# A fourth buffer for the tail's turned contexts, and a reordered last stage, in a two-layer cross-attention kernel

## The chip, the cores and the metric

The kernel runs on one core of a Trainium2 chip, in one launch. The metric is the device time of that launch in microseconds. Three runs of the kernel before took 968.51, 970.0 and 969.3 us: the median is 969.3 us. All times below are in microseconds unless another unit is named; times inside the launch count from the start of the profiled span.

A core has five engines with queues of their own, each working in the order of its queue: TensorE (PE in the profile, its weight loads PEld), VectorE (DVE), ScalarE (ACT), GpSimd (POOL) and SyncE (SP). SP computes nothing; it issues most of the DMA transfers. ACT and POOL can issue transfers too. Sixteen DMA engines carry them all.

## The reference

The model is two layers over 16 batches of 112 rows of 256 numbers, with a context of 375 rows of 256 for each batch. All inputs are float32 except int8 weights at the very end.

```
x = x + attention16(layernorm(x), ctx, Wq, Wk, Wv, Wo) + bo      # 16 heads of 64
x = x + routed_ffn(layernorm(x)) + shared_ffn(layernorm(x))      # top-1 of 2 experts, 1024 hidden
e = layernorm(x) @ ctx.T / 16 - (1 - mask) * 1e9                 # one head, keys and values are ctx
x = x + softmax(e) @ ctx
n = layernorm(x)
x_scale = max(max|n| / 127, 1e-5)                                # over ALL rows of all batches
q = clip(round(n / x_scale), -128, 127)
x = x + (q @ weight_int8.T) * x_scale * weight_scale + bias
```

The last layer can't be finished for any batch before the maximum over all 16 batches is known: `x_scale` is one number for everything. This comparison and what follows it form the end of the kernel.

## The kernel before, in words

**Stages.** The first attention runs in 64 units (16 batches times 4 groups of heads). Beside it, in the free places of the units, the feed-forward layer and the second attention of batches 0 to 7 are done. Routing sorts the rows by expert in two halves; the second half of the rows is sorted at the end of the first attention and computed in eight slots of 128 rows. Units are numbered on: the slots are units 70 to 77 (`FIRST_RUN` = 70), then the steps of the tail begin, `STEP_0` = 82, in which batches 8 to 15 (`TAIL` = 8) pass through the second attention and the last norm. `at(u, f, ...)` puts a call at the end of unit u, `mid(u, ...)` in its middle; calls of one unit keep the order in which they were put. This order is written out by hand, and each engine's queue follows it.

**Slots.** In each slot unit `slot_run` computes 128 rows with one expert's weights and `slot_store` (L823) stores the result, `yrow`, to the sorted array `y_s` in DRAM, on SP's queue. The last slot is unit 77. Units 78 to 81 hold the four quarters of the shared layer's last chunk (`quarter(6, i)`, `acc_sh` and `ph_sh` in the profile), which keep TensorE busy to 901.3. Then `shared_store` (L804) writes that chunk's rows to DRAM on SP's queue, and `load_xs` (L809) loads the rows of batches 13, 14 and 15 from there, one each in steps 0, 1 and 2.

**Gathers.** For each tail batch `sort_get` (L829) gathers its expert rows from `y_s` into `got`, an indirect DMA issued by POOL. It must wait for all eight slots' stores. The gathers of batches 8 to 11 come in steps -4 and -3, one right behind the other on POOL, then `sort_add` (L843) on POOL adds them, and `norm` follows: statistics on DVE (L271, L272), root on POOL (L275, L276), negated mean on POOL (L286), the normed rows `xn` on ACT (L300).

**A batch in the tail.** `stages(k)` writes step k for all batches that are under way; batch b = 8 + k is the one whose scores are computed in step k. Its own steps are:

- `second_1`, one step ahead: TensorE turns the normed rows (`pt_x`, L327), ACT copies them to `xT2` (L330).
- `second_2`, step k: TensorE computes the scores `pe` (L857) from `xT2` and the turned context `ctxT2`; ACT scales and masks them to `e` (L862), DVE finds the maxima (L871), ACT takes the exponentials (L878).
- `second_3`, a step later: the probabilities are turned (`pp`, L460).
- `second_4`, two steps later: TensorE multiplies them by the natural context `ctx_nat` (`pa`, L888), DVE adds the result to x (L897). Then come the statistics of the last norm (`l3`).
- three steps later: the rows of the last norm on ACT, and `third_max`: DVE's largest absolute value of the batch (`amax`, L925) and POOL's addition of the bias (L928).
- four steps later: `third_turn` turns these rows into `x3T`, the operand of the last product.

**Contexts.** `load_ctxT2` (L128 to L130) loads a batch's turned context, 128 partitions of 750 numbers, 375 KB; `load_ctx` (L119) loads the natural one, 125 partitions of 3 times 256 numbers, also 375 KB. Both are issued by SP. `late(pool, 2, n, ...)` gives the tail n buffers: three for `ctxT2`, five for `ctx_nat`. Batches 8, 9 and 10 are loaded at the end of units 75, 76 and 77, each pair behind that unit's `slot_store`; step k of the tail then loads batch 11 + k (`do(-3, ...)`, from step 0). A load waits, at the head of SP's queue, until its buffer's former reader is done: batch b's turned context reuses the buffer of batch b - 3. In unit 83 (step 1) SP also loads `x3T` of batches 0 to 7 (L1244, 896 KB), which were turned earlier and kept in DRAM.

**The end.** In step 9 (`k == B - TAIL + 1`) DVE reduces the maxima of batches 0 to 14 to `amax1`. Batch 15, the last, is compared by a short way on DVE (`farthest`, L314 to L317) without waiting for its normed rows; L1331 joins the two, TensorE turns the column (`pm`, L1333), DVE takes the maximum of the line (`top`, L1335), TensorE broadcasts it (`pb`, L1338), DVE makes `xscale` and `rscale` (L1340, L1342). Between `pm` and `pb` stand two idle products (`keep_warm(2)`, L1231), which only keep TensorE busy. After that comes the last call of `stages`, step 10, which turns batch 14's columns and writes batch 15's normed rows, and `third_turn` for batch 15.

Then the 16 batches are quantised in eight pairs: `scaled` multiplies by `rscale` and adds a constant that rounds, on ACT (L1355) for pairs 1, 3, 5, 6, 7 or on DVE (L1357) for pairs 0, 2, 4; `products` takes the constant off again to bf16 `xi` on ACT (L1362) and multiplies (`pf`, L1366); `stored` multiplies by the scales on DVE into `y` (L1377, four buffers), adds x on DVE for pairs 2, 5, 7 or on POOL for the others (L1385), and SP stores the pair (L1386). `y` of pair p reuses the buffer of pair p - 4 and so waits for that pair's store to land.

Of the kernel before, what the change touches and what calls it, by code (L numbers as in the profile page):

```python
# [19 lines left out]
P = 128  # L20
B, S, D = 16, 112, 256
SK = 375
# [4 lines left out]
DC = D // P  # L27
# [27 lines left out]
TAIL = 8  # L55
# [3 lines left out]
def tile_kernel(  # L59
# [26 lines left out]
    nc = tc.nc  # L86
# [4 lines left out]
    ctxp = ctx.enter_context(tc.tile_pool(name="ctx", bufs=2))  # L91
# [10 lines left out]
    def gen(name):  # L102
        return ps_gen.tile([P, 512], F32, tag="gen", name=name)
# [13 lines left out]
    ctx_nat, ctxT, ctxT2 = {}, {}, {}  # L117
# [8 lines left out]
        dma.dma_start(out=ctxT[b], in_=ctx_t[b])  # L126

    def load_ctxT2(b):  # L128
        ctxT2[b] = late(ctxp, 2, 3, [P, DC, SK], "ctxT_2", f"ctxT2_{b}")
        nc.sync.dma_start(out=ctxT2[b], in_=ctx_t[b])  # L130

    def weight(src, name, dma, pool=wpool):
# [112 lines left out]
    def late(pool, bufs, more, shape, tag, name):  # L245

        pool, bufs = (fin[0], more) if fin else (pool, bufs)
        return pool.tile(shape, F32, tag=tag, name=name, bufs=bufs)
# [73 lines left out]
    def transposed(dst, src, name):  # L322

        pt = gen(f"pt_{name}")
        n = src.shape[0]
        for c in range(DC):
            nc.tensor.transpose(  # L327
                pt[:, c * n : (c + 1) * n], src[:, c * P : (c + 1) * P], ident[:n, :n]
            )
        nc.scalar.copy(dst, pt[:, : DC * n].rearrange("p (c s) -> p c s", c=DC))  # L330
# [523 lines left out]
    def second_2(b, between=lambda: None):  # L854
        pe = gen(f"pe_{b}")
        for dc in range(DC):
            nc.tensor.matmul(  # L857
                pe[:S, :SK], xT2[b][:, dc, :], ctxT2[b][:, dc, :], start=(dc == 0), stop=(dc == DC - 1)
            )
        e = late(tmp, 1, 2, [S, SK], "e", f"e_{b}")  # L860
        if b >= TAIL:
            nc.scalar.activation(  # L862
                e, pe[:S, :SK], AF.Identity, bias=negb[:, b : b + 1], scale=ESCALE
            )
        else:
            nc.vector.tensor_scalar(e, pe[:S, :SK], ESCALE, negb[:, b : b + 1], ALU.mult, ALU.add)
        between()
        nmax = small.tile([S, 1], F32, tag="nmax2", name=f"nmax2_{b}")
        if b >= TAIL:

            nc.vector.tensor_reduce(nmax, pe[:S, :SK], AX.X, ALU.max)  # L871
            nc.vector.tensor_scalar(
                nmax, nmax, -ESCALE, negb[:, b : b + 1], ALU.mult, ALU.subtract
            )
        else:
            nc.vector.tensor_reduce(nmax, e, AX.X, ALU.max, negate=True)
        den = small.tile([S, 1], F32, tag="den2", name=f"den2_{b}")
        nc.scalar.activation(e, e, AF.Exp, bias=nmax, accum_out=den)  # L878
        rdens[b] = den
        es[b] = e  # L880
# [32 lines left out]
    def third_turn(bs):  # L913
        for b in bs:
            if b < TAIL:
                t = tmp.tile([P, DC, S], F32, tag="x3s", name=f"x3s_{b}", bufs=1)
                transposed(t, normed["l3", b], f"x3_{b}")
                nc.scalar.dma_start(out=x3T_d[b], in_=t)
            else:
                transposed(x3T[0][:, b, :, :], normed["l3", b], f"x3_{b}")  # L920

    def third_max(bs):
        for b in bs:
            if b < B - 1:
                nc.vector.tensor_reduce(  # L925
                    amax[:, b : b + 1], normed["l3", b], AX.X, ALU.max, apply_absolute_value=True
                )
            nc.gpsimd.tensor_tensor(xs[b], xs[b], bias_bc[:S], ALU.add)  # L928
# [84 lines left out]
    STEP_0 = FIRST_RUN + NT // 2 + 5  # L1013
# [4 lines left out]
    def at(u, f, *a):  # L1018
        extra[u].append((f, a))
# [85 lines left out]
    for b in range(TAIL):  # L1105
        at(u - 2 - (b > 0), sort_get, b)
        at(u - 4, load_xs, b)
        at(u - 2, load_ctxT2, b)
        at(u - 1, load_ctx, b)
        mid(u - 1, sort_add, b)  # L1110
        mid(u, second_1, b)
        at(u, second_2, b)
        mid(u + 1, second_3, b)
        at(u + 1, second_4, b)
        at(u + 1, third_norm, [b])
        mid(u + 3, third, [b])
        u += 1
# [44 lines left out]
    for b in range(TAIL, B):  # L1162

        at(FIRST_RUN + 3 if b < 13 else STEP_0 + b - 13, load_xs, b)
    for i in range(3):
        at(STEP_0 - 7 + i, load_ctxT2, TAIL + i)
        at(STEP_0 - 7 + i, load_ctx, TAIL + i)

    make_kT(0, 0, True)
    for i in range(GB):  # L1170
# [56 lines left out]
    def keep_warm(count):  # L1227

        pi = gen("warm")
        for _ in range(count):  # L1230
            nc.tensor.matmul(pi[:, :P], ident, ident, start=True, stop=True)  # L1231
# [22 lines left out]
    def stages(k):  # L1254
        def b_of(back):
            b = TAIL + k - back
            return b if TAIL <= b < B else None

        def do(back, f):
            b = b_of(back)  # L1260
            if b is not None:
                f(b)

        def norm_steps(name, b):
            nb_on = nc.gpsimd if name == "l2" or b == B - 1 else nc.vector
            steps[name, b] = norm([b], name, True, nb_on)
            for f in steps[name, b][:3]:
                f()

        def now(f, at_k):  # L1270

            for b, own in zip(range(TAIL, B), at_k):
                if own == k:
                    f(b)

        def rows(name):
            return lambda b: steps[name, b][3]()

        no = None
        stats = lambda b: norm_steps("l2", b)  # L1280
        now(sort_get, (-4, -4, -3, -3))
        now(sort_add, (-3, -3, no, no, 1, 2, 3, 4))
        now(stats, (-2,))
        now(rows("l2"), (-1,))
        yield
        now(sort_add, (no, no, -2, -1))
        now(stats, (no, -2))
        if k == -1:
            now(rows("l2"), (no, -1))
            do(-1, second_1)  # L1290
        do(0, lambda b: second_2(b, lambda: do(-1, second_1)))
        do(4, lambda b: third_turn([b]))
        do(1, second_3)
        do(3, rows("l3"))
        now(rows("l2"), (no, no, 0, 1, 2, 3, 4, 5))
        do(2, second_4)
        if k == B - TAIL + 1:

            amax1.append(const.tile([S, 1], F32, tag="amax1", name="amax1"))
            do(3, lambda b: third_max([b]))  # L1300
            nc.vector.tensor_reduce(amax1[0], amax[:, : B - 1], AX.X, ALU.max)
        do(2, lambda b: norm_steps("l3", b))
        now(sort_get, (no, no, no, no, -1, 0, 1, 2))
        now(stats, (no, no, -1, 0, 1, 2, 3, 4))
        if k >= 0:
            do(-3, load_ctxT2)
            do(-3, load_ctx)
        if k != B - TAIL + 1:
            do(3, lambda b: third_max([b]))
        yield  # L1310

    for u in range(NU + 3, LAST - 1):
        for f, a in middle[u]:
            f(*a)
            pump(2)
        k = u - STEP_0
        part = stages(k)
        next(part)
        for f, a in extra[u]:
            f(*a)  # L1320
            pump(2)
        if k >= B - TAIL:
            keep_warm(4)
        next(part)
# [8 lines left out]
    nc.tensor.transpose(pm[:1, :S], amax1, ident[:S, :S])  # L1333
    top = const.tile([1, 1], F32, tag="top", name="top")
    nc.vector.tensor_reduce(top, pm[:1, :S], AX.X, ALU.max)  # L1335
    keep_warm(2)
    pb = gen("pb")
    nc.tensor.matmul(pb[:, :1], ones[0:1, :], top, start=True, stop=True)  # L1338
    xscale = const.tile([P, 1], F32, tag="xscale", name="xscale")
# [4 lines left out]
    for _ in stages(LAST - 1 - STEP_0):  # L1344
        pass
# [5 lines left out]
    def scaled(pair):  # L1351
        t = x3T[0][:, 2 * pair : 2 * pair + 2, :, :]

        if pair % 2 or pair == 6:
            nc.scalar.activation(t, t, AF.Identity, bias=rounding, scale=rscale)  # L1355
        else:
            nc.vector.tensor_scalar(t, t, rscale, ROUND, ALU.mult, ALU.add)  # L1357
# [17 lines left out]
    def stored(pair):  # L1375
        y = fin[0].tile([S, 2, D], F32, tag="y", name=f"y_{pair}", bufs=4)
        nc.vector.tensor_tensor(  # L1377
            y,
            pfs[pair][:S, : 2 * D].rearrange("p (j d) -> p j d", j=2),
            wsx.unsqueeze(1).to_broadcast([S, 2, D]),  # L1380
            ALU.mult,
        )
        first = xs_place[2 * pair]
        add = nc.vector if pair in (2, 5, 7) else nc.gpsimd
        add.tensor_tensor(y, y, xall[:S, first : first + 2, :], ALU.add)  # L1385
        nc.sync.dma_start(  # L1386
            out=out[2 * pair : 2 * pair + 2].rearrange("b s d -> s b d"), in_=y
        )

    NP = B // 2  # L1390
    scaled(0)
    scaled(1)
    for pair in range(NP + 1):
        if pair < NP:
            products(pair)
        if pair + 2 < NP:
            scaled(pair + 2)
        if pair > 0:
            stored(pair - 1)
# [59 lines left out]
```

## Time and profile before

| | us |
|---|---|
| median of three runs | 969.3 |
| the profiled execution's own time | 970.18 |
| its span, first to last instruction | 968.4 |
| TensorE busy in the span | 925.2 (96%) |
| DVE, ACT, POOL busy | 494.3, 465.9, 463.8 |
| granted TensorE clock, mean of the span | 0.986 |

TensorE is busy nearly throughout; its idle time lies at the end. A table of that end by stretches, from the trace (busy time of TensorE, granted clock, share of the DMA engines):

| stretch | long | PE busy | clock | DMA share |
|---|---|---|---|---|
| 880 to 890 | 10 | 10.00 | 1.00 | 0.57 |
| 890 to 900 | 10 | 9.71 | 1.00 | 0.29 |
| 900 to 907 | 7 | 5.48 | 1.00 | 0.35 |
| 907 to 920 | 13 | 6.70 | 0.90 | 0.88 |
| 920 to 930 | 10 | 9.81 | 0.79 | 0.53 |
| 930 to 940 | 10 | 9.33 | 1.00 | 0.17 |
| 940 to 950 | 10 | 5.38 | 0.74 | 0.00 |
| 950 to 968 | 18 | 6.00 | 0.69 | 0.33 |

How the page and the trace's answers are read: a line of the timeline or of the queue of SP has the start, the duration, the engine, the line of the kernel, the operation, the tiles (out<-in) and how often; in square brackets stands how long the engine was idle before and who ended that. A line of the chain of waits has start, duration and what the time went to. A line of a stretch has its bounds and length, then the busy time of PE, PEld, DVE, ACT and POOL with the number of their instructions, then the granted TensorE clock as a share of full speed, the mean busy share of the 16 DMA engines, and GB/s. In the page's slices each digit is a fortieth of the span, in tenths.

### The profile page before, as it was taken

What the parts mean: (1) busy time and instruction counts of PE and PEld (TensorE: products, weight loads), DVE (VectorE), ACT (ScalarE), POOL (GpSimd) and SP (SyncE); (2) the same over time, 40 slices, a digit from 0 to 9 for tenths busy, and PEclk for the clock granted to TensorE, in tenths of its full rate; (3) what the DMA queues carried; (4) which work ended last, traced back from release to release, by engine and by line L of the source; (5) the groups of instructions that cost most, each with busy time, mean ns of one, the idle gap of its engine ahead of it and who ended that gap; (6) DMA issues with size and microseconds to landing.
All of it is one profiled execution on the core that took longest, in us unless ns stands there. A gap on an engine that the chain in (4) does not pass through costs nothing. (4 is left out here: it accounts for less than half of the span.)

```text
span 968.4 us, 16839 instructions
## 1 busy us (share of the span) xinstructions
PE 925.2 (96%) x5567; PEld 706.4 (73%) x5567; DVE 494.3 (51%) x1276; ACT 465.9 (48%) x1241; POOL 463.8 (48%) x504
## 2 busy tenths in 40 slices
PE   8999999999999999999999999899999999999683
PEld 5677677777777777778778787667767678899462
DVE  5655855464545444653444434577576442322464
ACT  4766565366535554564353442554545641221453
POOL 4766664366536544553242334666555622201743
PEclk9999999999999999999999999999999999999996
DMA  5654543243326422332645522645335720586522
GB/s 185 161 164 95 136 129 74 71 101 92 74 74 197 121 70 52 77 83 59 217 159 179 205 50 70 161 127 139 95 77 133 201 59 30 201 325 220 151 96 76
DMA packets 119911, 120.69 MB, mean 125 GB/s; under 512 B 15807, under 2 KB 107153, under 8 KB 115089
## 3 DMA queue, kind: packets, MB, share of 16 engines
q1 hardware_dynamic: 107664, 97.52, 35.8%
q10 hardware_dynamic: 8144, 11.20, 4.0%
q0 software_dynamic: 4016, 10.90, 3.7%
q8 instruction: 45, 0.74, 0.3%
q14 instruction: 42, 0.34, 0.1%
HBM read 71.19 MB, written 10.62 MB: 84 GB/s over the span
## 5 line engine op out<-in xcount | busy, mean ns | idle before, releaser
L455 POOL TENSOR_SCALAR p<-p,rden 128x375 f32<-128x375 f32 x256 | 315.1, 1244 | 258.4 <-DVE rden L452 251.3
L443 ACT ACTIVATE p<-sc,nmax 128x375 f32<-128x375 f32 x256 | 143.4, 571 | 174.9 <-DVE nmax L434 169.6
L338 PE MATMUL pk<-ctxT,wk 128*128 128x375 f32 x512 | 192.1, 497 | 4.3 <-ACT kT L347 2.3
L359 PE MATMUL pv<-wv,ctxT 128*128 128x256 f32 (+1 forms) x768 | 187.0, 380 | 0.4 <-ACT kT L347 0.4
L359 PEld LDWEIGHTS pv<-wv,ctxT 128*128 128x128 f32 (+1 forms) x768 | 143.3, 187 | 47.9 <-ACT kT L347 1.6
L504 ACT COPY pT<-blk 32x384 f32<-32x384 f32 x256 | 130.0, 508 | 29.2 <-DMA pT<-blk 26.9
L476 DVE STREAM_TRANSPOSE blk<-p 128x384 f32<-128x384 f32 x256 | 132.2, 552 | 7.4 <-POOL p L455 4.5
L338 PEld LDWEIGHTS pk<-ctxT,wk 128*128 128x128 f32 x512 | 90.3, 191 | 55.7 <-issue 9.9
L434 DVE TENSOR_REDUCE nmax<-sc 128x2 f32<-128x750 f32 x128 | 111.8, 911 | 0.6 <-PE sc L426 0.5
L514 PEld LDWEIGHTS pa<-pT,v 128*64 128x64 f32 (+1 forms) x1536 | 74.4, 136 | 33.3 <-issue 15.8
L426 PE MATMUL sc<-kT,qT 64*128 64x375 f32 x512 | 98.1, 501 | 0.0
L514 PE MATMUL pa<-pT,v 128*64 128x112 f32 (+1 forms) x1536 | 88.3, 263 | 2.2 <-DMA pT<-blk 1.4
L372 DVE COPY v<-pv 119x256 f32<-119x256 f32 x64 | 27.0, 423 | 122.5 <-PE pv L359 101.3
L347 ACT COPY kT<-pk 128x375 f32<-128x375 f32 x128 | 61.3, 479 | 47.0 <-PE pk L338 47.0
L426 PEld LDWEIGHTS sc<-kT,qT 64*128 64x128 f32 x512 | 43.9, 186 | 34.1 <-issue 13.5
L770 DVE TENSOR_SCALAR hT_sl<-ph_sl,slot_b 128x128 f32<-128x128 f32 x64 | 22.3, 349 | 69.3 <-PE ph_sl L760 69.3
L760 PE MATMUL ph_sh<-ffn_x,sw 128*128 128x256 f32 x224 | 56.0, 381 | 0.0
L747 PE MATMUL acc_sh<-sw,hT_sh 128*128 128x256 f32 x224 | 55.5, 379 | 0.3 <-ACT hT_sh L772 0.3
L395 PE MATMUL pq<-xT,wq 128*128 128x224 f32 x256 | 54.2, 354 | 0.0
L772 ACT ACTIVATE hT_sl<-ph_sl,slot_b 128x128 f32<-128x128 f32 x64 | 23.2, 367 | 60.6 <-PE ph_sl L760 49.2
L443 ACT ACTIVATION_READ_ACCUMULATOR p<-sc,nmax 128x1 f32 x256 | 51.8, 202 | 0.0
L542 PE MATMUL po<-wo,oT 128*128 128x256 f32 x224 | 50.8, 380 | 0.1
(221 smaller groups left out, 1148.1 us busy)
## 6 DMA issues: line engine op xcount, KB each, us to landing
pT<-blk SPq DMA_DIRECT2D x732, 48.0 KB
ctxT<-in_ctx_t SPq DMA_DIRECT2D x31, 375.0 KB
ctx<-in_ctx SPq DMA_DIRECT2D x16, 375.0 KB
ew<-in_w ACTq DMA_DIRECT2D x2, 1024.0 KB
x_s<-idle POOLq DMA_DIRECT2D x2, 1024.0 KB, 5.8
sw<-in_sw ACTq DMA_DIRECT2D x2, 1024.0 KB
row<-x_s SPq DMA_DIRECT2D x16, 128.0 KB
y_s<-yrow SPq DMA_DIRECT2D x16, 128.0 KB
```

The costliest lines, as they stand in the source:

```text
L338: nc.tensor.matmul(pk[:, :SK], wk_sb[:, dc, m * P : (m + 1) * P], ctxT[b][:, dc, :], start=(dc == 0), stop=(dc == DC - 1),)
L347: nc.scalar.copy(t, pk[:, :SK])
L359: nc.tensor.matmul(pv[: KP[c], n * UD : (n + 1) * UD], ctxT[b][:, dc, c * P : c * P + KP[c]], wv_sb[:, dc, k * UD : (k + 1) * UD], start=( ...
L426: nc.tensor.matmul(sc[:, j, :SK], qT[g, m][r, i * P : (i + 1) * P], kT[b, m][r, :], start=True, stop=True,)
L434: nc.vector.tensor_reduce(nmax, sc[:, :, :SK], AX.X, ALU.max, negate=True)
L443: nc.scalar.activation(p[:, :SK], sc[:, j, :SK], AF.Exp, bias=nmax[:, j : j + 1], accum_out=den[:, j : j + 1])
L455: nc.gpsimd.tensor_scalar(p, p, rden[:, j : j + 1], None, ALU.mult)
L476: nc.vector.transpose(blocked[u][:, :, h * 32 : (h + 1) * 32], probs[u][h].rearrange("p (n k) -> p n k", k=32),)
L504: nc.scalar.copy(pT[r, :, i, :], of[r, :, i, :])
L514: nc.tensor.matmul(pa[j * DH : (j + 1) * DH, j2 * S : (j2 + 1) * S].rearrange("p (i q) -> p i q", q=QB), vv[b, k][: KP[c], c, h * DH : (h ...
L747: nc.tensor.matmul(self.acc[:n, i, :D], hT[:, i * n : (i + 1) * n], self.wb[:, f, :], start=(f == 0), stop=(f == FC - 1),)
L760: nc.tensor.matmul(ph[:, : self.n], self.wa[:, dc, f * P : (f + 1) * P], self.src[:, dc, :], start=(dc == 0), stop=(dc == DC - 1),)
```

## The change

There are five edits.

1. `ctxT2` has four buffers instead of three.
2. The first four batches' contexts are loaded ahead of the tail instead of the first three: batches 8 and 9 in unit 75, batches 10 and 11 in unit 76. In the steps, batch 12 + k is loaded in step k (`do(-4, ...)`), so batch b's turned context reuses the buffer of batch b - 4.
3. Batch 14's columns are turned in step 9, right behind the reduction of the maxima, instead of in step 10 behind `pb`.
4. The two idle products between `pm` and `pb` are gone.
5. ACT scales pairs 2 to 7 and DVE pairs 0 and 1. Of the last additions DVE makes those of pairs 4 and 7, POOL the other six.

```diff
     def load_ctxT2(b):
-        ctxT2[b] = late(ctxp, 2, 3, [P, DC, SK], "ctxT_2", f"ctxT2_{b}")
+        ctxT2[b] = late(ctxp, 2, 4, [P, DC, SK], "ctxT_2", f"ctxT2_{b}")
...
-    for i in range(3):
-        at(STEP_0 - 7 + i, load_ctxT2, TAIL + i)
-        at(STEP_0 - 7 + i, load_ctx, TAIL + i)
+    for i in range(4):
+        at(STEP_0 - 7 + i // 2, load_ctxT2, TAIL + i)
+        at(STEP_0 - 7 + i // 2, load_ctx, TAIL + i)
...
-        do(4, lambda b: third_turn([b]))
+        if k < B - TAIL + 2:
+            do(4, lambda b: third_turn([b]))
...
             nc.vector.tensor_reduce(amax1[0], amax[:, : B - 1], AX.X, ALU.max)
+            do(3, lambda b: third_turn([b]))
...
-            do(-3, load_ctxT2)
-            do(-3, load_ctx)
+            do(-4, load_ctxT2)
+            do(-4, load_ctx)
...
-    keep_warm(2)
     pb = gen("pb")
...
-        if pair % 2 or pair == 6:
+        if pair > 1:
             nc.scalar.activation(t, t, AF.Identity, bias=rounding, scale=rscale)
...
-        add = nc.vector if pair in (2, 5, 7) else nc.gpsimd
+        add = nc.vector if pair in (4, 7) else nc.gpsimd
```

## The prediction

> **What bounds the kernel now.** All times are microseconds from the start of the span. I read the page's slices first, then the chain of waits over the last 70 us, then the order of issue on SP's queue, then stretches of a few microseconds. The slices say where TensorE is not the bound: only in the last three or four.
>
> ```profile
> PE   8999999999999999999999999899999999999683
> PEclk9999999999999999999999999999999999999996
> DMA  5654543243326422332645522645335720586522
> ```
>
> Up to 901 TensorE is full with matmuls that the change leaves alone, so everything is decided behind that. The chain of waits there names two places:
>
> ```profile
> 889.87 0.04 POOLq L829
> 890.75 0.86 POOL got L829
> ...
> 901.32 0.21 PE pt_x L327 x2
> ...
> 907.11 12.69 DMA ctxT<-in_ctx_t
> ...
> 946.05 0.88 PE warm L1231 x4
> 946.93 0.51 PE pb L1338 x2
> ```
>
> First, POOL's gathers (L829) wait until 889.87; that is the landing of the last slot's store, by the trace's semaphore events at 889.80. Second, the scores of batch 12 (pe, L857) wait for its turned context: TensorE stands idle 5.67 and runs pe in 2.81 instead of 1.5, because its granted clock was 0.50 from 917.4 to 924.3. Batch 11's pe starts at 911.02 and batch 13's at 925.39, two steps in 14.4 where the next ones (925.39, 929.22, 933.18) take 3.9 each: 6.6 are lost here. SP's queue in order of time shows who stands in front of whom:
>
> ```profile
> 873.60 0.43 SPq L130 DMA_DIRECT2D ctxT<-in_ctx_t  x1
> 874.08 0.37 SPq L121 DMA_DIRECT2D ctx<-in_ctx  x1
> 880.47 0.35 SPq L823 DMA_DIRECT2D y_s<-yrow  x1
> 880.85 0.43 SPq L130 DMA_DIRECT2D ctxT<-in_ctx_t  x1
> 881.64 0.28 SPq L121 DMA_DIRECT2D ctx<-in_ctx  x1
> 887.49 0.33 SPq L823 DMA_DIRECT2D y_s<-yrow  x1
> ...
> 905.26 0.38 SPq L130 DMA_DIRECT2D ctxT<-in_ctx_t  x1
> 905.68 0.33 SPq L121 DMA_DIRECT2D ctx<-in_ctx  x1
> ```
>
> The store issued at 880.47 lands only at 885.45: eleven of its sixteen parts at 882.0 to 882.2, the other five from 883.89 on, each behind the ctx load issued at 874.08, which lands at 885.18. So a ctx load (125 partitions) sits on five of the sixteen DMA engines, and what is issued later waits behind it there. The stretches show those five alone at work, a share of 0.32:
>
> ```profile
> 884.40:885.40 1.00, 1.00 (x10) 0.95 (x9) 0.00 (x0) 0.37 (x1) 0.00 (x0) 1.00 0.32 107
> 885.60:888.40 2.80, 2.80 (x15) 2.46 (x14) 0.83 (x2) 0.47 (x1) 0.00 (x0) 1.00 0.32 111
> ```
>
> **The fourth buffer: what goes.** With four buffers batch 12's load needs batch 8's buffer, goes out in step 0 and takes the place on SP's queue that batch 11's has now. It no longer stands behind the 896 KB of x3T (906.58). The wait of 5.67 and the slow clock behind it go: at most the 6.6 above.
>
> **What the moved loads add.** Each issue counts: in unit 75 now ctxT and ctx of batches 8 and 9, in unit 76 of 10 and 11, all ahead of the last slot's store in unit 77. Today two pairs lie ahead of that store, then four. On the slowest of the five engines the landings (885.45, 886.32, 889.46, 889.80) price a pair at 0.87 for ctxT and 3.14 for ctx, 4.0 together; two pairs are 8.1. The store lands at 889.80 + 8.1 = 897.9 and the first gather starts 0.95 later, at 898.85 instead of 890.75. Behind it on POOL come, in order, three more gathers (1.25 each) and the adds and norms of batches 8 and 9, so these move by the whole 8.1. Batch 9's normed rows on ACT end at 909.0 instead of 900.93, and the copy of batch 8's turned rows is behind them in ACT's order: pe of batch 8 starts at 909.4 instead of 901.95, 7.5 late. The cover that hid the gathers so far is the last quarter of the shared layer, which ends at 901.31; only about 0.6 of it is left over.
>
> The Trainium skill, "DMA: Bandwidth & Descriptors", says in "Queues, rings and completion order" that each DMA engine takes descriptors in the order of its ring, and in "Why a DMA increments its semaphore by 16 and not by 1" that the number of engines divides the partitions, so 125 give five; both speak against moving these loads ahead of a store that is waited for. At its 27 GiB/s an engine a ctx load would take an estimated 2.65 instead of the 3.14 measured, two pairs 7.0, and the forecast below would be 1.1 lower; the row decides.
>
> **Slow clock.** TensorE idles from 901.3 to 907. An idle of 5.67 brought 0.50 for 6.8 before; I charge 1.8 here (pe 2.81 for 1.5, the transposes beside it), bounded by 1.3 (that pe alone) and 3.4 (half of 6.8). Batch 12 follows batch 8 by the 9.1 from 901.95 to 911.02, one step of 3.9, and this 1.8: 924.2, and batch 13 at 928.1 against 925.39 now. Paced by TensorE batch 15 starts at 935.9, against 933.18: **+2.7**, so 6.6 of gain against 9.3 of delay.
>
> **The new wait on SP.** The load of batch 12 waits for the end of pe of batch 8, 912.2, and it is queued at 905.26 today. Behind it on SP stand ctx of 12, the rows of batch 14, x3T, batch 13's pair, the rows of batch 15. Batch 15's rows land at 923.57 today, so at 930.6. From there: POOL's add 0.9, its norm, rows and transpose 4.0 (926.67 to 930.69 today), from that transpose to pe 2.5 (930.69 to 933.18): pe of batch 15 at 938.0, **+4.8**. Today this chain has 2.2 to spare. The lower bound: batch 11's load took 4.51 from issue to landing, batch 10's 2.96, so the stream may be 1.55 quicker, +3.3. I take +4.5, near the top, since the gathers that slowed the one load move along with it.
>
> **The end.** The two idle products lie between the maximum and its broadcast: top is ready at 946.35, pb starts at 946.87, so 0.5 goes. They held no clock up:
>
> ```profile
> 944.80:946.80 2.00, 1.09 (x5) 0.93 (x5) 0.98 (x5) 0.00 (x0) 0.75 (x2) 0.50 0.00 0
> 951.00:954.90 3.90, 3.76 (x18) 3.72 (x19) 2.52 (x5) 3.90 (x9) 1.77 (x2) 0.50 0.02 4
> ```
>
> The clock is 0.50 with them too, so I price their loss at nothing else. The page "TensorE: Matmul & The Clock Gate", "Part 1: The HAM clock gate", makes idle stretches of 3.4 costly and so speaks for such products; by it losing them could cost up to 0.3, half of pb's 0.58.
>
> Batch 14's transposes, copy and the wait behind them today hold up ACT until 948.29, where the rows of batch 15 start though their bias is ready at 945.65. With them done before, ACT has batch 15's rows by 946.3, its copy at 947.6 and the first xi (L1362) at 947.9 instead of 950.52, as ACT's scaling of pair 1 (0.76) is gone from before it too. The transposes cost nothing: TensorE has 3.26 idle before pm. Without that idle they would cost 0.4. From xi the end follows by the store chain: y 1.8 later, four adds on POOL of 1.29 each, the output's landing 2.35, since y has four buffers, then y 0.69 and DVE's add 1.1 of pair 7; its store goes out at 960.0 against 962.54, a gain of 2.5. If instead ACT sets the end, eight xi (0.47) and six scalings (0.65) from 947.9 end at 955.6 against 956.95, a gain of 1.35. I take **-2.4**: today the chain runs through the output's landing and not through ACT. The sixth add on POOL and the fourth pair on DVE's side are within it.
>
> **Sum.** +4.5 - 2.4 = +2.1. The profiled execution took 970.18 (span 968.4), so 972.3; it lies 0.9 above the median of 969.3, so the median becomes **971.4**.
>
> **Rivals.** *TensorE's pace decides* (18%): batch 15's rows land before 928.5, when they no longer matter; then +2.7 - 2.4 = +0.3, 969.6. For it speaks the clean start of the stream, against it that all its pieces are in one queue. *The store is not held up* (22%, the other side): one mechanism, the five engines at 885 to 898. If the later loads were spread over other engines, or the store overtook them, the gathers would start at 890.75 as now; batch 13's pe would start at 919.9, batch 15's by its rows at 931.0, -2.2, and with the end -4.6: 964.7. It decides from a landing before about 895.5, a delay of 5.5 instead of 8.1, below which nothing is lost. Against it speaks the store at 880.47. That the fourth buffer does not do what it says is covered by the wait on batch 8: the load goes out late, though no longer last.
>
> **Numbers.** Forecast 60%, with its own range from 970.0 (969.3 + 3.3 - 2.6) to 973.8 (+4.8 - 1.35, and 1.0 of the 1.6 by which the slow clock's bound of 3.4 exceeds my 1.8). A measurement here can tell about 0.2%, 1.9, from no change. Slower than 971.2: two thirds of the forecast, as that part of its range lies above, and a tenth of the first rival, 0.43. Within 967.4 to 971.2: the rest of these two, 0.35. Faster: the second rival, 0.22. The range 967.0 to 973.8 leaves out most of the second rival and little else.
>
> **What would show it.** Right: POOL's first gather near 899; TensorE idle after 901 for some 6; no wait of pe for ctxT at batch 12; POOL waiting for x<-x_d near 930; xi 2.7 instead of 5.1 after the maximum (L1331). Wrong: a gather before 895, or pe of batch 15 before 934.

## The result, and the profile after

The changed kernel takes 974.51 us (median of 7 runs, 972.48 to 978.54), the kernel before beside it 968.51 (7 runs, 965.91 to 970.0): the ratio is 1.0068, with a 95% interval of 1.0044 to 1.0092. The change makes the kernel slower by 6.0. The prediction had the direction (slower as the likeliest case), with 2.1 instead of 6.0; the time lies 0.7 above the high end of its range.

The profiled execution of the changed kernel took 973.39, with a span of 971.7. The page's slices come first (a fortieth of the span each, in tenths), the same three rows as those shown of before:

```profile
PE   9999999999999999999999999999999999998773
PEclk9999999999999999999999999999999999999897
DMA  5664543243327422332646522555335521795522
```

By its digits the granted clock is lower in the 38th slice now (899 to 923), where before had no lower digit ahead of the last slice. SP's queue shows the moved loads (start, duration of the issue, line, tiles):

```profile
871.64 4.19 SPq L130 DMA_DIRECT2D ctxT<-in_ctx_t  x1
875.87 0.35 SPq L121 DMA_DIRECT2D ctx<-in_ctx  x1
878.60 2.13 SPq L823 DMA_DIRECT2D y_s<-yrow  x1
...
881.92 3.84 SPq L130 DMA_DIRECT2D ctxT<-in_ctx_t  x1
885.80 0.34 SPq L121 DMA_DIRECT2D ctx<-in_ctx  x1
886.25 3.63 SPq L823 DMA_DIRECT2D y_s<-yrow  x1
```

An issue that took 0.35 to 0.43 before now takes up to 4.19: SP itself is held while transfers ahead are unfinished. (What ends such a hold the traces do not show.) The last store is issued at 886.25. By the trace's semaphore events eleven of its sixteen parts land at 891.1 to 891.5 and the other five from 895.77 on, the last at 896.57. Before, issue and landing were 2.31 apart, now 10.32, and this is the first of two long transfers in the chain of waits (start, duration, what the time went to):

```profile
886.25 10.32 DMA y_s<-yrow
...
902.84 0.44 DVE bn_l L271
...
903.91 5.07 PE acc_sh L747 x12
...
909.61 1.53 PE pe L857 x4
...
919.22 11.44 DMA x<-x_d
...
930.78 0.73 POOL x L843
...
935.60 1.01 PE pt_x L327 x4
...
937.24 2.15 PE pa L888 x6
```

The first line is the delay that the prediction expected. The third was not in it: twelve matmuls of the shared layer (`acc_sh`) stand *behind* the gathers, at 5.07; the run with the split alone, below, has the same twelve at 2.59. The stretches of the changed kernel (bounds, length, busy time of PE, PEld, DVE, ACT and POOL, granted clock, DMA share, GB/s) show the hole ahead of them:

```profile
892.00:896.00 4.00, 4.00 (x20) 3.43 (x19) 0.00 (x0) 0.00 (x0) 0.00 (x0) 1.00 0.30 103
896.00:900.00 4.00, 0.30 (x2) 0.00 (x0) 0.00 (x0) 0.00 (x0) 2.04 (x3) 1.00 0.09 29
900.00:904.00 4.00, 0.09 (x1) 0.09 (x1) 1.12 (x4) 0.00 (x0) 3.48 (x6) 0.66 0.28 86
904.00:908.00 4.00, 4.00 (x9) 2.80 (x10) 0.74 (x3) 1.56 (x3) 3.45 (x8) 0.50 0.00 0
```

TensorE stops at 896.3 in the middle of the shared layer and stands for 7.6; then nine matmuls fill 4.00 at a clock of 0.50. DVE's instructions in order of time tell why (in brackets the idle time before, and who ended it):

```profile
902.84 0.43 DVE L271 BATCH_NORM_STATS2 bn_l<-x 112x6 f32<-112x256 f32 x1 [12.93 <-POOL x L843]
903.31 0.18 DVE L272 BATCH_NORM_AGGREGATE mv_l<-bn_l 112x2 f32<-112x6 f32 x1
903.40 0.45 DVE L770 TENSOR_SCALAR hT_sh<-ph_sh,sb 128x256 f32<-128x256 f32 x1
```

The statistics of batch 8 (L271) stand ahead of the shared layer's `hT_sh` (L770) in DVE's queue. They wait 12.93 for POOL's sum, which waits for the gathers; `hT_sh`, whose input has long been there, waits with them, and so do the matmuls that read it.

The end did as expected. From the joined maximum to the first `xi` it is 951.41 to 953.95, 2.54; before, 945.42 to 950.52, 5.10:

```profile
951.41 0.22 DVE L1333 SCALAR_TENSOR_TENSOR amax<-far,y_l,amax 112x1 f32<-112x1 f32 x1
...
952.39 0.51 PE L1339 MATMUL pb<-top,ones 1*128 1x1 f32 x2 [0.35 <-DVE top L1337]
...
953.95 0.58 ACT L1363 ACTIVATE xi<-x3T 128x448 bf16<-128x448 f32 x1
```

**Where the 6.0 come from.** Profiled executions reach the last slot at different times though the kernels do the same work up to there: the issue of the last slot's second weights lies between 869.86 and 873.76 in the fourteen profiles of this study. The table counts from that issue (872.70 before, 869.86 after). The columns: POOL's first gather; the start of pe of batch 8; from there to pe of batch 15; from there to `pm`; from `pm` to the end of the span; the sum; and the median of the runs. All rows but the first two are experiments of the next section: *split* is the whole change with each context load cut into two pieces, *split alone* the kernel before with the same. A row's stretches are from one execution; its median is from several, and the experiments have runs of the kernel before of their own (968.15 to 968.87).

| kernel | gather | pe 8 | to pe 15 | to pm | to end | sum | median |
|---|---|---|---|---|---|---|---|
| before | 18.05 | 29.25 | 31.23 | 12.53 | 22.69 | 95.7 | 968.51 |
| the whole change | 27.49 | 39.75 | 29.62 | 12.55 | 19.92 | 101.8 | 974.51 |
| loads only | 27.37 | 40.00 | 29.97 | 12.47 | 22.13 | 104.6 | 978.63 |
| end only | 17.47 | 29.01 | 29.76 | 12.56 | 20.07 | 91.4 | 965.59 |
| store first | 18.44 | 32.84 | 27.44 | 12.56 | 20.04 | 92.9 | 967.79 |
| store on ACT's queue | 20.74 | 35.52 | 29.79 | 13.44 | 19.89 | 98.6 | 972.22 |
| norms behind | 27.44 | 38.40 | 27.65 | 12.55 | 19.96 | 98.6 | 973.43 |
| rows early | 27.62 | 40.77 | 26.12 | 12.61 | 19.83 | 99.3 | 973.19 |
| split | 22.67 | 35.50 | 24.76 | 12.55 | 20.04 | 92.9 | 966.49 |
| split, rows early | 21.51 | 34.65 | 25.48 | 12.55 | 19.97 | 92.7 | 967.68 |
| split alone | 17.43 | 28.68 | 26.64 | 12.45 | 22.72 | 90.5 | 964.41 |
| split and end | 17.52 | 28.79 | 26.93 | 12.55 | 19.87 | 88.1 | 962.41 |
| split, store first | 17.72 | 30.45 | 25.32 | 12.56 | 19.78 | 88.1 | 961.83 |
| buffer only | 18.26 | 29.48 | 31.15 | 12.53 | 22.57 | 95.7 | 970.43 |

Before against after: +10.5 up to pe of batch 8, -1.6 from there to pe of batch 15, -2.8 behind `pm`; +6.1 together, against 6.0 between the medians. One execution can be trusted this far: *end only* and *buffer only* keep the order of the loads of before, and from pe of batch 8 to pe of batch 15 they take 29.76 and 31.15, where before has 31.23. So the -1.6 there is hardly more than what executions differ by. The first gather repeats better (17.47 to 18.26 in these three, 27.37 to 27.62 in the four kernels that have the whole change's loads and the store behind them on SP's queue), and so does the end. That the sums meet the medians to 0.1 is partly luck: for loads only the sums differ by 8.9, the medians by 9.8.

### The profile page after: what moved, and what is told of

It reads as the page before. It is cut to its first block, busy times and chain, and to the rows that moved or that the text cites. A ratio compares the mean times of both kernels' runs of the same rounds, so it can differ in the third digit from the quotient of the medians.

```text
span 971.7 us, 16829 instructions
## 1 busy us (share of the span) xinstructions
PE 925.6 (95%) x5563; PEld 704.7 (73%) x5563; DVE 493.4 (51%) x1274; ACT 466.9 (48%) x1242; POOL 464.0 (48%) x505
## 3 DMA queue, kind: packets, MB, share of 16 engines
q10 hardware_dynamic: 8144, 11.20, 3.9%
## 5 line engine op out<-in xcount | busy, mean ns | idle before, releaser
L747 PE MATMUL acc_sh<-sw,hT_sh 128*128 128x256 f32 x224 | 57.5, 390 | 7.6 <-DVE hT_sh L770 7.6
L770 DVE TENSOR_SCALAR hT_sl<-ph_sl,slot_b 128x128 f32<-128x128 f32 x64 | 22.3, 350 | 70.2 <-PE ph_sl L760 70.2
L747 PEld LDWEIGHTS acc_sh<-sw,hT_sh 128*128 128x128 f32 x224 | 43.7, 196 | 14.8 <-DVE hT_sh L770 8.0
```

What stands on the lines that cost most here:

```text
L747: nc.tensor.matmul(self.acc[:n, i, :D], hT[:, i * n : (i + 1) * n], self.wb[:, f, :], start=(f == 0), stop=(f == FC - 1),)
```

## The experiments

All were timed in five rounds, the last (buffer only) in three, with runs of the kernel before on the same chip: 968.86 as the median for the first four, 968.87 for the next four, 968.15 for the last four.

**The parts alone.** Loads only has edits 1 and 2, end only edits 3 to 5, as in the diff of the change.

> Edits 1 and 2 alone (fourth buffer, moved loads), the end as before. Theory (the last slot's store stands behind four context pairs on five DMA engines, gathers late, and DVE's norms of batch 8 hold up the shared layer): the loss without the end's gain, +8.9, about 977.4 against 968.5. Rival (the reordered end costs the time): about 968.5 or less.

Measured: 978.63, ratio 1.0098 (1.007 to 1.0126).

> Edits 3, 4 and 5 alone (batch 14 turned earlier, no idle products, scaling six pairs on ACT), loads as before. Theory: from L1331 to the end of the span 20.3 instead of 23.0, so -2.7, about 965.8. Rival (the reordered end costs the time): above 970.

Measured: 965.59, ratio 0.9977 (0.9959 to 0.9994). The parts add up: +9.8 and -3.3 make +6.5, against 6.0 for both. In the table the loads cost everything ahead of pe of batch 8, and the end gains 2.6 behind `pm`. (The 1.5 by which *end only* is shorter between pe of batch 8 and pe of batch 15 lies in work that edits 3 to 5 leave alone.) So the rest of the study is on the loads.

**The store ahead of the loads.** The pairs of batches 10 and 11 go out in unit 77, behind the last store, so that two pairs lie ahead of it as before.

```diff
-        at(STEP_0 - 7 + i // 2, load_ctxT2, TAIL + i)
-        at(STEP_0 - 7 + i // 2, load_ctx, TAIL + i)
+        at(STEP_0 - 7 + min(i, 2), load_ctxT2, TAIL + i)
+        at(STEP_0 - 7 + min(i, 2), load_ctx, TAIL + i)
```

> The changed kernel with one load pair in units 75 and 76 and the pairs of batches 10 and 11 behind the last slot's store in unit 77. Theory: the first gather starts about 3.3 after that store is issued, TensorE goes through the shared layer without the gap of 7.6, pe of batch 12 finds its context, batch 15's rows decide; -4.6 against before, about 964. Rival (it is the number of early loads, not their place): two pairs behind the store slow the gathers instead, 970 or more.

Measured: 967.79, ratio 0.9987 (0.9972 to 1.0002), between the two expectations and not to be told from the kernel before. This takes back most of the loss, so the place of the loads ahead of the store is most of what costs. Yet pe of batch 8 is still 3.6 late. The chain of waits of this run shows it:

```profile
891.56 6.41 DMA got<-y_s,batch_place
...
901.86 3.48 PE acc_sh L747 x8
```

The store lands 2.69 after its issue, but now the gathers themselves are slow, 6.41 from issue to landing. In the run with the split alone (below), where one pair is issued behind the store, the same gather lands 2.73 after its issue. Here two natural contexts are issued behind the store, on five engines, and by the semaphore events five parts of this gather come at 897.40 to 897.97, while ten were in by 894.67.

**Another queue for the store.** All loads as in the whole change; the last slot's store is issued by ACT.

```diff
-        nc.sync.dma_start(out=s.y[i * P : (i + 1) * P, :], in_=y)
+        last = s is sorts[1] and i == outer_first(s)[-1]
+        (nc.scalar if last else nc.sync).dma_start(out=s.y[i * P : (i + 1) * P, :], in_=y)
```

> The changed kernel with the last slot's store issued by ACT, on another queue; the four pairs stay ahead of it. Theory (order within SP's queue on five engines): the store no longer waits for them, first gather within 5 of the end of the last slot instead of 11, about 964 to 966. Rival (the five engines' bandwidth, whatever the queue): gather as late as in the changed kernel, 974.

Measured: 972.22, ratio 1.0034 (1.0021 to 1.0047): a miss. The store goes out unhindered, while SP is stuck on its loads. The two issues, on ACT's queue and on SP's, in that run:

```profile
888.56 0.33 ACTq L824 DMA_DIRECT2D y_s<-yrow  x1
```

```profile
885.36 4.47 SPq L130 DMA_DIRECT2D ctxT<-in_ctx_t  x1
```

Eleven parts land at 890.11 to 890.26, the five others at 893.55 to 893.68, 5.12 after the issue. So leaving the queue takes away half of the 10.32, and what is left above the 2.31 of before is work on the five engines, whichever queue it comes from. The Trainium skill, "DMA: Bandwidth & Descriptors", "Queues, rings and completion order", has a rule for it: a DMA engine takes turns between the queues that have work for it. That agrees with a store that lands later than in the kernel before (2.31) and earlier than behind everything on one queue (10.32). The gathers behind it are slow again (5.74 in the chain).

**The order on DVE.** In the whole change, the statistics and normed rows of batches 8 and 9 are put behind the last quarter of the shared layer.

```diff
-        now(stats, (-2,))
-        now(rows("l2"), (-1,))
...
-        now(stats, (no, -2))
+        now(stats, (-1, -1))
...
-            now(rows("l2"), (no, -1))
+            now(rows("l2"), (-1, -1))
```

> The whole change, with the statistics and the normed rows of batches 8 and 9 put behind the last quarter of the shared layer on DVE and ACT, instead of ahead of it. Theory (the order of DVE's queue stops the shared layer when the gathers are late): the idle time of 7.6 inside acc_sh goes, acc_sh is done by about 901 to 904 of the profile, and TensorE's idle time comes after it; pe of batch 8 starts 2 to 3 earlier than in the changed kernel, 971.5 to 973. Rival (the gap costs nothing, since the gathers alone set when batch 8 can start): pe of batch 8 as in the changed kernel, 974 to 975.5.

Measured: 973.43, ratio 1.0049 (1.0034 to 1.0065). TensorE in that run:

```profile
907.52 0.64 PE L327 MATMUL pt_x<-ident,xn_l 112*128 112x112 f32 x2 [8.82 <-ACT xn_l L300]
909.04 2.84 PE L857 MATMUL pe<-ctxT,xT 128*112 128x375 f32 x4 [0.89 <-ACT xT L330]
```

The hole of 7.6 in `acc_sh` is gone, so its cause, the order on DVE and ACT, is shown. But an idle time of 8.82 behind the shared layer has taken its place, pe of batch 8 comes only 1.35 earlier, and it runs at half clock, 2.84 instead of 1.52. The median is 1.1 below that of the whole change, between the two expectations, and the two intervals overlap. Most of the delay is the gathers' own.

**The five engines.** The natural contexts of batches 8 to 15 are loaded in two pieces, partitions 0 to 111 and 112 to 124, on sixteen and thirteen engines. The bytes and the order stay.

```diff
-        nc.sync.dma_start(out=t, in_=ctx_in[b].rearrange("(c p) d -> p c d", p=KC))
+        rows_ctx = ctx_in[b].rearrange("(c p) d -> p c d", p=KC)
+        if b < TAIL:
+            nc.sync.dma_start(out=t, in_=rows_ctx)
+        else:
+            nc.sync.dma_start(out=t[:S], in_=rows_ctx[:S])
+            nc.sync.dma_start(out=t[S:KC], in_=rows_ctx[S:KC])
```

First with the whole change:

> The whole change, with each natural context of batches 8 to 15 loaded as two transfers, partitions 0 to 111 and 112 to 124, so that sixteen and thirteen DMA engines carry it instead of five. Same bytes, same order on SP's queue, one more issue (0.3 to 0.4) per context. Theory (the five engines, not the order of the queue, hold up the last store): a context costs about what its turned twin of equal size costs, 0.9 to 1.2 instead of 3.14, so all four pairs have landed before the last store is issued, the store lands within 3 of its issue, the first gather starts some 9 earlier than in the changed kernel (about 890 in the frame of the kernel before) and the gathers take about 2.7 again; no gap of 7.6 inside acc_sh; batch 15's rows land 6 to 9 earlier than in the changed kernel; 962 to 966. Rival (what holds the store is the order of the queue and the amount of bytes, whoever carries them): the store still lands 8 to 10 after its issue, 973 to 976.

Measured: 966.49, ratio 0.9978 (0.9959 to 0.9997), 0.5 above the theory's range. The five engines are about half of it: the store now lands 5.47 after its issue, a miss against the 3 expected, and the first gather is 4.8 earlier than in the whole change but 4.6 later than before. The hole in `acc_sh` shrinks from 7.6 to 2.36 and 0.86, but does not go. Of the 4.6, 3.2 are the longer landing (5.47 against 2.31). The other 1.5 are a later issue, 16.33 after the last weights against 14.79: SP waits for earlier transfers. Its issues at 884.28, 885.88, 887.18 and 888.76 each come 0.01 to 0.02 after the landing of the transfer that it issued eight places earlier, and a split context takes one place more. For the longer landing the amount of bytes is left as the cause, which is argued from two rows and not from a run of its own. The stretch ahead of the last store in this run:

```profile
884.00:888.00 4.00, 4.00 (x28) 3.74 (x27) 0.78 (x3) 0.73 (x2) 0.00 (x0) 1.00 1.11 263
```

The share is 1.11 at 263 GB/s: all sixteen engines are full with the four pairs, where the whole change had 0.30 and 103 GB/s in its stretch 892 to 896. With the split and two pairs ahead (below) the store lands 1.73 after its issue. The second gain is behind pe of batch 8: from there to pe of batch 15 it is 24.76 instead of 29.62, as the contexts and rows of the tail stream faster too.

Then the split in the kernel before, with nothing of the change:

> The kernel before with the same split of the natural contexts alone. Theory: the store now lands at 889.80, 2.3 after its issue, so the five engines take little from it (0 to 0.5); the wait of pe of batch 12 for its turned context stays, since that load is issued late, though less by what the natural contexts of batches 11 and 12 take from it; 966 to 969. Rival (the split is worth as much without the change as with it): 960 to 963.

Measured: 964.41, ratio 0.9952 (0.9936 to 0.9967): a miss by 1.6 on the good side. The store's landing gains little, as expected (gather 17.43 against 18.05 in the table). The wait of pe of batch 12 for its turned context shrinks from 5.67 to 1.85, and with it goes the half clock. The kernel before, then this run:

```profile
919.94 2.81 PE L857 MATMUL pe<-ctxT,xT 128*112 128x375 f32 x4 [5.67 <-DMA ctxT<-in_ctx_t]
```

```profile
916.57 1.49 PE L862 MATMUL pe<-ctxT,xT 128*112 128x375 f32 x4 [1.85 <-DMA ctxT<-in_ctx_t]
```

The other two kernels with before's loads have waits of 3.94 (end only) and 4.45 (buffer only), each with a pe of 2.81 behind it. So half or more of the wait that the fourth buffer was to remove was the five engines' too.

**Two pairs ahead, with the split.** Split and end has three buffers and the loads where they were before, with edits 3 to 5. Split, store first has the whole change, the split, and the order of "store first".

> The kernel before with the natural contexts of batches 8 to 15 split over sixteen and thirteen engines, and edits 3 to 5 (the end) of the change; three buffers, loads where they were. Theory: the split alone took 964.4 and the end alone 965.6 where the kernel before took 968.9; they lie in different stretches, so their gains of 4.5 and 3.3 add up: 960.5 to 962. Rival (after the split the end hangs on something else, and the gain of the end shrinks): 963 to 965.

> The whole change with the split contexts, and the pairs of batches 10 and 11 issued in unit 77 behind the last slot's store, not in unit 76. So the fourth buffer is kept, and ahead of that store lie two pairs, as in the kernel before. Theory (what costs is the bytes ahead of the store; the fourth buffer itself is worth something, the 1.85 of wait of pe of batch 12 that the split alone leaves): store lands within 3 of its issue, first gather at 890.5 to 892 in the frame of the kernel before, 959.5 to 961.5, up to 2 better than split and end without the fourth buffer. Rival (the two pairs behind the store now share the engines with the gathers, as they did without the split): gathers take over 4 instead of 2.7, pe of batch 8 2 to 4 late, 962 to 965.

Measured: 962.41, ratio 0.9933 (0.991 to 0.9957), and 961.83, ratio 0.9934 (0.9912 to 0.9957). Both are faster than both kernels; each is 0.3 to 0.4 above the range that its theory gave. The chain of waits of the second:

```profile
886.37 1.73 DMA y_s<-yrow
...
889.01 6.22 DMA got<-y_s,batch_place
...
899.11 1.99 PE acc_sh L752 x8
```

(With the split the kernel's lines behind it lie five further down.) The store lands after 1.73, where the whole change needs 10.32. But the gathers are slow again, as the rival said (6.22 against 2.73), now behind two pairs on sixteen engines, and pe of batch 8 is 1.7 later than with split and end. pe of batch 12 waits for nothing, and the way to pe of batch 15 is 1.6 shorter. The two cancel: the fourth buffer with its earlier loads is not shown to be worth anything on top of the split.

**The rows of the last batches.** The whole change without the split, with the rows of batches 14 and 15 loaded in unit 82.

```diff
-        at(FIRST_RUN + 3 if b < 13 else STEP_0 + b - 13, load_xs, b)
+        at(FIRST_RUN + 3 if b < 13 else STEP_0, load_xs, b)
```

> The whole change, contexts not split, with the rows of batches 14 and 15 loaded at the end of unit 82, with batch 13's, ahead of x3T and of batch 13's contexts. Theory (the prediction's step: the rows of batch 15, at the end of SP's queue, set when batch 15 starts, and TensorE's pace would allow 2 to 5 earlier): POOL's wait of 3.7 for x<-x_d goes, 970 to 972.5. Rival (TensorE's pace or the contexts decide, the rows are a wait beside them): the time of the whole change, 973.5 to 975.5.

Measured: 973.19, ratio 1.0051 (1.0032 to 1.007), between the two expectations and within the interval of the whole change. In the trace POOL's wait of 3.68 for the rows goes, and pe of batch 15 comes 26.12 after that of batch 8, not 29.62. The chain shows what is last now:

```profile
926.03 12.50 DMA ctxT<-in_ctx_t
938.66 1.50 PE pe L857 x4
```

Batch 15's turned context takes 12.50 from issue to landing. It came this late in the whole change too: it lands 66.8 after the issue of the last weights here and 66.3 there, where pe of batch 15 started only at 69.4, because of the rows. So batch 15's start hangs on the whole stream on that queue; its rows were only the piece that was needed last, and behind them the context left little to gain.

With the split the same edit shows nothing:

> The whole change with the split contexts, and the rows of batches 14 and 15 loaded at the end of unit 82, with batch 13's, instead of one and two units later. Theory: with the gathers on time batch 15's start hangs on its rows, at the end of SP's queue; with them ahead of x3T and of batch 13's contexts TensorE's pace decides, 960 to 964, 1 to 3 faster than the split alone. Rival (TensorE's pace decides already with the split alone): the same time as the split alone, within 1.

Measured: 967.68, ratio 0.9985 (0.9968 to 1.0002), against 966.49 for the whole change with the split, 1.2 more, with intervals that overlap: nearest to the rival's case. The rows are not what batch 15 waits for there: in both traces POOL's sum for it waits only 0.2 to 0.4, for a gather.

**The buffer alone.**

```diff
-        ctxT2[b] = late(ctxp, 2, 3, [P, DC, SK], "ctxT_2", f"ctxT2_{b}")
+        ctxT2[b] = late(ctxp, 2, 4, [P, DC, SK], "ctxT_2", f"ctxT2_{b}")
```

> The kernel before with four buffers for the turned contexts and nothing else: edit 1 without edit 2. Theory (the wait of pe of batch 12 comes from the place of its load on SP's queue, behind x3T, and no load waits long for a buffer): 968 to 969.7, no difference. Rival (the buffer itself frees the queue): 963 to 967.

Measured: 970.43, ratio 1.0026 (1.0011 to 1.0041), 0.7 above the range of no difference; its stretches sum to 95.7 like those of before, so no mechanism for a loss shows. But the profiled execution, at 967.84, is the quickest of the ten, and whether there is a loss stays open. pe of batch 12 still waits 4.45 for its context:

```profile
916.62 2.81 PE L857 MATMUL pe<-ctxT,xT 128*112 128x375 f32 x4 [4.45 <-DMA ctxT<-in_ctx_t]
```

So the buffer frees nothing by itself. The earlier place on SP's queue is what takes the wait away, and that place is what costs.

## Why the prediction was wrong, step by step

- *The moved loads hold up the last store*: right, and the largest term. Predicted 8.1 on the first gather, measured 9.4 (27.49 against 18.05). By the semaphore events the third and fourth pair end on the slowest of the five engines at 887.47, 891.89 and 896.28, 4.4 each, where 4.0 was read from the trace of before; two pairs are 8.8. (Twice 4.0 would have been 8.0, not the 8.1 of the prediction.) The rest is in the stream ahead of them and was not taken apart.
- *"The cover that hid the gathers so far is the last quarter of the shared layer, which ends at 901.31; only about 0.6 of it is left over"*: this step failed. The prediction took TensorE's work up to 901.31 as fixed ("Up to 901 TensorE is full with matmuls that the change leaves alone") and let only batch 8 be late. But DVE has the statistics of batch 8 ahead of that layer's `hT_sh`, so late gathers stop the cover itself. The chain of waits of the kernel *before* shows it, in lines that the prediction left out:

```profile
895.49 0.75 POOL x L843
896.26 0.44 DVE bn_l L271
...
897.33 0.57 POOL y_l L276
...
898.82 0.46 ACT hT_sh L772
...
899.32 1.99 PE acc_sh L747 x8
```

  The chain runs from the gathers through the norm into the shared layer, so nothing was left over even before. In place of a credit of 0.6 the chain from the first gather to pe of batch 8 grew by 1.1 (12.26 against 11.20), with matmuls at a clock of 0.50. pe of batch 8 came 10.5 late where 7.5 was predicted: 3.0, of which 1.3 are the store's and 1.7 this step's. With the order on DVE and ACT changed (norms behind), pe of batch 8 came 1.35 earlier.
- *Slow clock*: the 1.8 was charged behind pe of batch 8. It fell in `acc_sh` ahead of it instead, so pe of batch 12 follows pe of batch 8 after 12.16, not the 14.8 predicted. A second spell was not foreseen: TensorE waits 2.60 ahead of pe of batch 14, and the clock is 0.68 from 934 to 938. From batch 15's turn (`pt_x`) to its scores it takes 3.63 there instead of 2.49.
- *The new wait on SP, +4.5 at pe of batch 15*: measured +8.9. The rows land 21.0 after pe of batch 8, where 21.2 was predicted, so this term was right, though in part by luck. The load of batch 12 was to go out 2.8 after the start of pe of batch 8, at its end with a half clock; pe of batch 8 took 1.53, and the load went out 2.76 after its start (912.37) because the rows of batch 13 stand ahead of it on SP (911.93) and wait for the store of the shared layer, which was late too. The surplus is the 3.0 from above and 1.4 behind it, 1.1 of which is that second slow spell. (The 1.4 is within the 1.5 that executions differ by in this stretch.) That the rows themselves decide was too narrow: with them early, the contexts do.
- *The end, -2.4*: -2.8 in the two profiles and -3.3 in the runs of the end alone.
- *Sum*: 2.1 and 3.0 and 1.4 and -0.4 are 6.1. Two slips change nothing in it: the terms listed for the new end add up to 959.0, not 960.0, as the first y's own 0.70 and the small waits are not among them, and with the wait of 6.6 gone batch 13's pe would start at 918.8, not 919.9.
- *Rivals*: that TensorE's pace decides was refuted by the chain of waits, which runs through the landing of batch 15's rows, and by *rows early*, where pe of batch 15 follows pe of batch 8 after 26.12 instead of 29.62. (POOL's wait for the rows by itself shows nothing: it is 3.68 now and was 4.20 before, with time to spare behind it.) That the store is not held up was refuted by its landing, and when it was made so (store first, without the split), the time fell to 967.8 and not to 964.7, as the gathers share the same five engines with the loads behind the store.

## What to carry to other kernels

Before pricing a delay against the work that covers it, look in the queues of all engines for anything that stands ahead of that work and waits for the late thing; a full TensorE is only cover if none of its inputs waits in order behind the delay. Before moving a load ahead of a store, count the bytes per DMA engine: a load whose partitions fall on five engines costs several times as much there as one on sixteen (3.14 against 0.87 for the same bytes), and splitting it into a multiple of sixteen and a remainder was worth 0.5% here (0.9936 to 0.9967) with no move at all. When a change of several edits costs time, run its parts alone: here the loads lost three times what the end gained.

## What the runs showed of the hardware that was not expected

- SP is held while its own transfers are unfinished, as early as unit 75: issues of 0.35 to 0.43 took 2.13 to 4.19. So the last store was also issued 1.6 later (16.39 against 14.79 after the last weights). With the contexts in two pieces (split) no issue there took over 0.76, but SP waited between them for earlier landings, and the store was 1.5 later all the same.
- A store on ACT's queue still landed 5.12 after its issue, against 2.31, with its last five parts 3.3 to 3.4 behind the other eleven: the five engines are shared between queues.
- POOL's gathers, short as they are, slow down behind loads. The first landed 2.73 after its issue behind one pair in pieces (split alone), 4.52 behind one with its context in one piece (before), 6.41 behind two of these (store first) and 6.22 behind two in pieces (split, store first): not only the five engines count, but the bytes too.
- Two pieces of one context took less than one. On the engine that finishes last, the third and fourth pair of the whole change took 4.4 each in one piece and 3.1 and 2.1 in two (889.05, 892.18, 894.30), with sixteen engines full (a share of 1.11).
- Executions that do the same work up to there reach the last slot up to 3.9 apart (869.86 to 873.76), 0.4% of the time. Stretches counted from a common instruction can agree far better (the first gather within 0.25 in four kernels), but not all do (1.5 between pe of batch 8 and pe of batch 15).
